# Second batch of the first layer: the transposed normalised input from VectorE, with moments spread as rows

## The chip, the cores and the metric

The kernel runs on one core of a Trainium2 chip. A core has five engines with queues of their own: TensorE (matrix products; the profile splits it into PE, the products, and PEld, the loading of weights), VectorE (DVE), ScalarE (ACT), GpSimd (POOL) and SyncE (SP), which issues nearly all DMA transfers here. Each engine works through its instructions in a fixed order and waits for semaphores. The metric is the device time of one launch in microseconds (us); lower is better.

## What is computed

Two layers over x of shape 4 x 512 x 256 (four batches, 512 tokens, 256 channels), all in float32. The parts that matter here, from the reference:

```python
xn = _layernorm(x)                          # (x - mean) / sqrt(var + 1e-5), per token
s  = _L0_attn_ref(xn, ...)                  # xn + rmsnorm(xn @ M) * norm_w, M made of W_in, W_out and a gain
g  = silu(_L0_ffn_ref(xn, W1, W2, W3))      # W2 . fwht(silu(W1 xn) * (W3 xn))
x  = x + s * g
xn = _layernorm(x)
s  = _L1_attn_ref(xn, ...)                  # a causal attention with a layernorm of its own
g  = silu(_L1_ffn_ref(xn, ...))             # as in the first layer
x  = x + s * g
```

In the first layer's mixer the recurrence is taken over a single step from a zero state, so it collapses into one 256 x 256 matrix M = W_in^T . diag(g) . W_out^T, with g a sum over B and C. The Walsh-Hadamard transform is folded into W2.

## The kernel before

**Arithmetic.** Products keep float32 accuracy by splitting each operand into a high and a low part (`split`, L59: a copy to the high part on ACT, a subtract to the low part on VectorE) and adding three products (`mm3`, L80). Transposes on TensorE are products with an identity in float32 (`transpose`, L77).

**Order of work.** The kernel is written as generators whose steps are handed to the slots of a feed-forward network (FFN). One FFN per layer and batch is the backbone: `ffn` (L466) in the first layer, 8 chunks of 128 hidden units. For each chunk c TensorE forms the up and gate products (tiles f_0gu, f_1gu and so on, the digit is the batch), ACT takes silu, VectorE multiplies (`gates`, L528), the result is split (L539) and the down products (f_0dn) follow. Behind each chunk come two slots (L548, L552), and `Beside` (L884) spreads the steps of the other work over the 16 slots. The order of instructions on each engine is then made by a planner from the written order, which comes with priorities, and a model of the durations; `after(ins)` (L463) binds the instructions of a block to a place behind `ins` on the same engine, without a wait of its own.

**The first batch** differs: its down products all stand behind the up products (defer = NH, L1042), for the W2 of the first layer is still being transformed (`prep_first`, L965) while the up products run. `prep_first` also loads the second batch's x (L981) and makes M (`prep_m`, L191, with tiles wg, wi, mps and m; the split of W_in into wi is L207). Its chunks 0 to 3 write their hidden into early tiles, and the low halves of these four are made later, two behind chunk 6 and two behind chunk 7 (L540 to L544).

**The work around the change.** In the FFN of the first batch the slots carry, in this order (L1007 to L1019): `prep_first` (12 steps left), `mixer(0)` (L716, 3 steps: two banks of xn @ M, then the RMS norm, which starts at L730, and the addition to xn) and `norm(0, 1)` (L430, 3 steps), the layernorm of the second batch:

- `layernorm` (L266): statistics (L275), aggregation (L277), the addition of eps (L279) on VectorE, the power -1/2 on POOL (L280), then xn of 4 token tiles on VectorE (L282).
- for each half k of the channels: 4 transposes of 128 x 128 on TensorE into a bank of PSUM (`transpose_half`, L288, tiles xt_1tp), then a split into the high and the low part of xT. These feed f_1gu, the up products of the second batch.

`first["xt"]` (L459) is the last of these transposes, and the down products of the first batch's chunks 6 and 7 are bound behind it (L559).

**Moments as rows.** The second layer knows another way already: in `norm` with layer = 1 (L436 to L455) `moments` (L254) gives the mean and the reciprocal deviation of each token as a tile mr of 128 x 8, one transpose on TensorE (mrp) turns it to 8 x 128, ACT copies it out (rows), SP writes it to DRAM (there) and reads it back spread over all 128 partitions (mrb, 128 x 2 x 512). VectorE then uses rows of it as operands on a transposed tile.

**Buffers.** Large tiles come from a ring of 10 buffers (`t4`, L44); x and the scratch of W2's transform share 4 (`x_slot`, L96). PSUM has 3 banks for "ms" (mps, o, w2ps, xt_1tp, mrp), 3 for "gu" and 2 for "dn".

Of the kernel before, what the change touches and what calls it, by code (L numbers as in the profile page):

```python
# [21 lines left out]
P = 128  # L22
# [13 lines left out]
def kernel(ctx: ExitStack, tc: tile.TileContext, a: dict, out: bass.AP):  # L36
# [154 lines left out]
    def prep_m(win, wout):  # L191

        cb = wp.tile([P, 4, 2, DS], F32, name="cb")
        nc.vector.tensor_tensor(cb, bc[:, :, 0:2, :], bc[:, :, 2:4, :], ALU.mult)
        cbd = wp.tile([P, 4, DS], F32, name="cbd")
        nc.vector.tensor_tensor(cbd, cb[:, :, 0, :], cb[:, :, 1, :], ALU.subtract)
        g = wp.tile([P, 4], F32, name="g")
        nc.vector.tensor_reduce(g, cbd, AX.X, ALU.add)
        wg = [t4(f"wg{i}", [P, 4, D], F32R) for i in "hl"]
        wi = [t4(f"wi{i}", [P, 4, D], F32R) for i in "hl"]  # L200
        for c in range(4):
            nc.scalar.mul(wg[0][:, c, :], wout[:, c, :], g[:, c : c + 1])
            nc.vector.scalar_tensor_tensor(
                wg[1][:, c, :], wout[:, c, :], g[:, c : c + 1], wg[0][:, c, :].bitcast(F32),
                ALU.mult, ALU.subtract,
            )
        split(win, *wi)  # L207
        yield
        hi, lo = (wp.tile([P, 2, D], F32R, name=f"m{i}") for i in "hl")
        o = psum("mps", [P, 2, D])  # L210
        for i in range(2):
            mm3(
                o[:, i, :],
                [(tuple(z[:, k, sl(i)] for z in wi), tuple(z[:, k, :] for z in wg)) for k in range(4)],
            )
        split(o, hi, lo)
        first["m"] = hi, lo
        yield
# [160 lines left out]
    def norm_first():  # L379
# [47 lines left out]
        first["norm"] = hi_, lo_  # L427
        yield

    def norm(layer, b):  # L430
        xn = act.tile([P, NT, D], F32, tag="xn", name=f"xn{layer}_{b}", bufs=3)
        xns[layer, b] = xn
        with after(first["gate"] if b > 1 - layer else None):
            first["scaled"] = layernorm(f"ln{layer}_{b}", xs[b], xn)
        yield
        if layer:  # L436


            mr = act.tile([P, 2, NT], F32, tag="mr", name=f"mr{b}", bufs=2)
            moments(f"ln2_{b}", xn, mr)  # L440
            yield
            o = psum(f"mrp{b}", [2 * NT, P], **DN[b == 0])
            transpose(o, mr.rearrange("p a t -> p (a t)"), ident)
            rows = act.tile([2 * NT, P], F32, tag="rows", name=f"rows{b}", bufs=1)
            with after(first["table"] if b else None):
                nc.scalar.copy(rows, o)
            there = dram.tile([2 * NT, P], F32, tag="rows", name=f"there{b}")
            nc.sync.dma_start(there, rows)
            mrb = t4(f"mrb{b}", [P, 2, S])
            nc.sync.dma_start(  # L450
                mrb, there.rearrange("(a t) p -> a (t p)", a=2).unsqueeze(0).to_broadcast([P, 2, S])
            )
            mrs[b] = mrb
            yield
            return  # L455
        hi, lo = xTs[0, b] = xt_pair(f"xt0_{b}")
        for k in range(2):
            o = transpose_half(f"xt0_{b}", xn, k)
            first["xt"] = line["last"]  # L459
            split(o, hi[:, k, :], lo[:, k, :])  # L460
            yield
# [4 lines left out]
    def ffn(name, xT, w13, w2, slot, defer=1, spare=(), parts=1, behind=False, tail=()):  # L466

        w2h, w2l = w2
        dn, outs, firsts = [], [], {}

        def down(c, hh, hl, tiles=range(NT)):
            if not dn:
                dn.extend(psum(f"{name}dn{i}", [P, 2, D], tag="dn", bufs=2) for i in range(2))
                outs.extend(dn[t // 2][:, t % 2, :] for t in range(NT))
            for t in tiles:
                o = outs[t]
                for n, (l, r) in enumerate(((hh, w2h), (hh, w2l), (hl, w2h))):  # L480
                    first = c == 0 and n == 0
                    stop = c == NH - 1 and n == 2

                    def one(start):
                        return matmul(
                            o, l[:, sl(t)], r[:, c, :], start=start, stop=stop, skip_group_check=True
                        )

                    if first and t % 2 == 1:
                        with tc.issue_after(firsts[t // 2].ins):
                            ins = one(False)
                    elif first:
                        ins = firsts[t // 2] = one(True)
                    else:
                        ins = one(False)
            return ins

        queue, gates, late = [], [], []  # L500
        for c in range(NH):
            with after(gates[-2] if behind and c >= 2 else None):
                wh, wl = w13(c // 2)
            gu = []
            for j in range(2):

                o = psum(f"{name}gu{c}_{j}", [P, S], **(DN[0] if behind and c == 1 else GU))
                cols = slice((c % 2) * D + j * P, (c % 2) * D + (j + 1) * P)
                gu.append((o, cols))
            for half in range(parts if c == 0 else 1):  # L510
                n = S // (parts if c == 0 else 1)
                ts_ = slice(half * n, (half + 1) * n)
                if parts == 1 or c:
                    for o, cols in gu:
                        last_up = mm3(o[:, ts_], k_pairs((wh, wl), cols, xT, ts_))
                    continue

                for n, (w, x) in enumerate(((wh, xT[0]), (wl, xT[0]), (wh, xT[1]))):
                    for o, cols in gu:
                        for k in range(2):  # L520
                            last_up = matmul(
                                o[:, ts_], w[:, k, cols], x[:, k, ts_],
                                start=n + k == 0, stop=n + k == 3,
                            )
            gu = [o for o, _ in gu]
            h = hid(f"{name}h{c}")
            first["silu"] = nc.scalar.activation(h, gu[0], AF.Silu)
            gates.append(nc.vector.tensor_tensor(h, h, gu[1], ALU.mult))  # L528
            first["gate"] = gates[-1]
            if c < len(spare):  # L530
                hh, hl = spare[c]
            else:
                hh = hid(f"{name}hh{c}", F32R)
                hl = hid(f"{name}hl{c}", F32R)
            if c < len(spare):
                nc.scalar.copy(hh, h)
                late.append((hl, h, hh))
            else:
                split(h, hh, hl)  # L539
            for _ in range(2 if c >= NH - 2 else 0):  # L540
                if late:
                    lo_, h_, hi_ = late.pop(0)
                    with after(gates[-1]):
                        nc.vector.tensor_tensor(lo_, h_, hi_.bitcast(F32), ALU.subtract)  # L544
            queue.append((c, hh, hl))
            ups = last_up if behind else None
            with after(gates[-1] if behind else None), after(ups):
                slot(2 * c)  # L548
            if len(queue) > defer:
                down(*queue.pop(0))  # L550
            with after(gates[-1] if behind else None), after(ups):
                slot(2 * c + 1)  # L552
        line["fixed"] = bool(tail)
        line["last"] = last_up
        for what in tail:
            what()
        for q in queue:

            with after(first.get("xt") if behind and q[0] >= NH - 2 else None):  # L559
                down(*q)  # L560
        return dn

# [153 lines left out]
    def mixer(b):  # L716
# [5 lines left out]
        for i in range(2):  # L722
# [4 lines left out]
            for t in (2 * i, 2 * i + 1):  # L727
                nc.scalar.activation(junk, osb[:, t, :], AF.Square, accum_out=r[:, t : t + 1])
            yield
        nc.vector.tensor_scalar(r, r, 1.0 / D, RMS_EPS, ALU.mult, ALU.add)  # L730
        nc.gpsimd.tensor_tensor(r, r, mhalf, ALU.pow)
        for t in range(NT):
            nc.vector.scalar_tensor_tensor(
# [182 lines left out]
    def call(f, *args):  # L916
        f(*args)
        yield


    NORM, MIXER, W2P = 3, 3, 12

# [82 lines left out]
    for b in range(B):  # L1005
        tasks = []
        if b == 0:  # L1007
            prep = prep_first()
            next(prep)
            tasks.append((prep, 12))  # L1010
        if b:
            tasks.append((call(gate_all, f"g0_{b - 1}", dn, xns[0, b - 1], xs[b - 1]), 1))
        tasks.append((mixer(b), MIXER))
        if b + 1 < B:
            if b:
                load_x(b + 1)
            if b == 2:
                tasks.append((prep_s(0), 4))
            tasks.append((norm(0, b + 1), NORM))  # L1019
        if b == 0:  # L1020
            early = w2_tile("early0"), w2_tile("early1")
            spare = [
# [175 lines left out]
```

## Time and profile before

| | us |
|---|---|
| median of 3 runs | 358.62 (358.52 to 358.67) |
| the profiled execution's own time | 358.58 |
| its span, first to last instruction | 356.8 |
| TensorE busy in it | 351.1 |
| VectorE busy | 287.1 |
| ScalarE busy | 197.8 |
| GpSimd busy | 20.8 |
| mean granted TensorE clock | 0.998 of full speed |

The span is what the trace covers; 1.78 us of the execution's own time lie around it. A busy share is an average over stages. The end of a matmul is modelled, since matmuls overlap in the array: how far apart two of them start says more than how long each is shown. In the tables of instructions in order of time the columns are the start in us, the length in us, the engine, the line, the operation, the written tile <- the read tiles, the shape (for TensorE contraction x output rows, then the moved operand), the count of merged instructions and, in brackets, idle time of the engine before it with what ended it. L70 is the helper through which all products go, so they are told apart by their tiles.

### The profile page before, as it was taken

The numbers are of one execution on the slowest core, as the hardware profiler recorded it, in microseconds if no ns is written. First come the engines' busy times: TensorE is split into PE (matmuls) and PEld (weight loads), VectorE is DVE, ScalarE is ACT, GpSimd is POOL, SyncE is SP. The second block draws the span as 40 slices with busy tenths as digits, with TensorE's granted clock in tenths as the row PEclk, the third lists the DMA queues.
The fourth block names the chain that finished last, engine by engine and source line by source line (L and its number), as shares of the span: only waits on it lengthen the run. The fifth ranks groups of instructions, "written<-read, shape, count | busy, mean of one in ns | idle before, by whom it ended". The sixth has DMA issues, their size and how long they took to land.

```text
span 356.8 us, 6274 instructions
## 1 busy us (share of the span) xinstructions
PE 351.1 (98%) x2477; PEld 327.5 (92%) x2477; DVE 287.1 (80%) x597; ACT 197.8 (55%) x373; POOL 20.8 (6%) x22
## 2 busy tenths in 40 slices
PE   8999999999999999999999999999999999999995
PEld 6878998888988898888999999999999999999994
DVE  6899659998579938998887957989679897577646
ACT  3666166265463425674467655586555676556443
POOL 2000110300020210100110001100011000000000
PEclk9999999999999999999999999999999999999999
DMA  7935000301044316656257145562554745445501
GB/s 232 349 96 201 2 1 2 116 2 61 0 162 168 145 38 229 251 180 195 114 208 263 36 174 208 216 224 93 206 202 150 227 163 206 141 157 184 198 2 59
DMA packets 16284, 52.25 MB, mean 146 GB/s; under 512 B 1632, under 2 KB 7936, under 8 KB 16256
## 3 DMA queue, kind: packets, MB, share of 16 engines
q1 hardware_dynamic: 15968, 51.60, 41.0%
q8 instruction: 19, 0.31, 0.4%
q10 hardware_dynamic: 288, 0.26, 0.2%
q14 instruction: 9, 0.07, 0.1%
HBM read 42.40 MB, written 9.45 MB: 145 GB/s over the span
## 4 chain that ended last, share of the span: by engine, by line
PE 98%; DVE 1%; ACT 0%; issue 0%
PE f_0dn L70 6%; PE f_1dn L70 6%; PE f_2dn L70 6%; PE f_0gu L70 6%; PE f_1gu L70 6%; PE f_2gu L70 6%; PE f_3gu L70 6%; PE f_3dn L70 6%; PE sc L70 4%; PE pv L70 4%; PE o L70 3%; PE v L70 3%; PE tq L70 3%; PE warm L70 2%; PE w2ps L70 1%; PE pt L70 1%
## 5 line engine op out<-in xcount | busy, mean ns | idle before, releaser
L70 PE MATMUL f_3gu<-xt,w 128*128 128x512 f32 x96 | 25.0, 396 | 0.0
L70 PE MATMUL f_2gu<-xt,w 128*128 128x512 f32 x96 | 24.8, 395 | 0.0
L70 PE MATMUL f_1gu<-xt,w 128*128 128x512 f32 x96 | 24.8, 395 | 0.0
L70 PE MATMUL f_0gu<-xt,w 128*128 128x512 f32 (+1 forms) x108 | 24.3, 378 | 0.0
L70 PEld LDWEIGHTS f_0gu<-xt,w 128*128 128x128 f32 x108 | 18.4, 188 | 4.4 <-issue 1.0
L70 PEld LDWEIGHTS f_1gu<-xt,w 128*128 128x128 f32 x96 | 17.0, 188 | 3.1
L70 PEld LDWEIGHTS f_2gu<-xt,w 128*128 128x128 f32 x96 | 17.0, 188 | 3.0
L70 PEld LDWEIGHTS f_3gu<-xt,w 128*128 128x128 f32 x96 | 17.0, 188 | 2.9
L61 ACT CAST f_2hh<-f_2h 128x512 fp32r<-128x512 f32 x16 | 10.0, 622 | 15.4 <-DVE f_2h L528 12.2
L70 PE MATMUL f_3dn<-w2l,f_3hh 128*128 128x256 f32 x64 | 17.7, 281 | 0.0
L70 PE MATMUL f_3dn<-w2h,f_3hh 128*128 128x256 f32 x64 | 17.7, 281 | 0.0
L70 PE MATMUL f_1dn<-w2l,f_1hh 128*128 128x256 f32 x64 | 17.7, 281 | 0.0
L70 PE MATMUL f_2dn<-w2h,f_2hh 128*128 128x256 f32 x64 | 17.7, 282 | 0.0
L70 PE MATMUL f_1dn<-w2h,f_1hh 128*128 128x256 f32 x64 | 17.6, 280 | 0.0
L70 PE MATMUL f_2dn<-w2l,f_2hh 128*128 128x256 f32 x64 | 17.6, 280 | 0.0
L70 PE MATMUL f_3dn<-w2h,f_3hl 128*128 128x256 f32 x64 | 17.0, 281 | 0.0
L70 PE MATMUL f_1dn<-w2h,f_1hl 128*128 128x256 f32 x64 | 17.0, 281 | 0.0
L70 PE MATMUL f_2dn<-w2h,f_2hl 128*128 128x256 f32 x64 | 16.7, 281 | 0.0
L61 ACT CAST f_3hh<-f_3h 128x512 fp32r<-128x512 f32 (+1 forms) x17 | 10.0, 594 | 10.1 <-DVE f_3h L528 5.9
L61 ACT CAST f_1hh<-f_1h 128x512 fp32r<-128x512 f32 x16 | 9.9, 622 | 9.7 <-DVE f_1h L528 6.6
L62 DVE TENSOR_TENSOR f_2hl<-f_2h,f_2hh 128x512 fp32r<-128x512 f32 x16 | 10.9, 684 | 4.5 <-ACT f_2hh L61 4.5
L62 DVE TENSOR_TENSOR f_3hl<-f_3h,f_3hh 128x512 fp32r<-128x512 f32 (+1 forms) x17 | 11.0, 654 | 3.7 <-ACT f_3hh L61 3.6
(487 smaller groups left out, 1147.3 us busy)
## 6 DMA issues: line engine op xcount, KB each, us to landing
sw<-s SPq DMA_DIRECT2D x32, 896.0 KB, 5.7
s<-sp SPq DMA_DIRECT2D x8, 512.0 KB, 4.1
s<-sp SPq DMA_DIRECT2D x8, 384.0 KB, 2.8
w2raw<-in_w SPq DMA_DIRECT2D x4, 512.0 KB, 5.3
sraw<-in_w SPq DMA_DIRECT2D x4, 512.0 KB, 3.2
mrb<-there SPq DMA_DIRECT2D x4, 512.0 KB, 3.6
w13raw<-in_w SPq DMA_DIRECT2D x3, 512.0 KB, 6.8
x<-in_x SPq DMA_DIRECT2D x3, 512.0 KB, 3.5
```

The costliest lines, as they stand in the source:

```text
L61: h = nc.scalar.copy(hi, src)
L62: return h, engine.tensor_tensor(lo, src, hi.bitcast(F32), ALU.subtract)
L70: ins = call(*args, **kwargs)
```

## The change

In the first layer's second batch, xT is no longer made by transposing xn on TensorE. The host hands over a transposed copy of that batch's x (`xT`, 2 x 128 channels on the partitions, 512 tokens). `norm_second` loads it (raw), computes the moments with `moments`, spreads them through `spread`, which is the second layer's code taken out of `norm`, and makes xT on VectorE by one subtract and one multiply over 128 x 1024, then one split. xn itself, which the mixer and the gate read, is still made from x, now behind the split.

The order moves with it: the moments are bound behind the low half of wi (`first["wi"]`), `prep_first`'s last two steps come behind them, and the steps of the mixer and of `norm_second` alternate. `first["xt"]` is now the transpose of the moments, and the down products of chunks 2 to 7 are bound behind it. The last two late low halves are bound behind the moments, the mixer's RMS behind the split (`first["second"]`).

```diff
-        split(win, *wi)
+        first["wi"] = split(win, *wi)[1]
...
+    def spread(name, o):
+
+        rows = act.tile([2 * NT, P], F32, tag="rows", name=f"rows{name}", bufs=1)
+        nc.scalar.copy(rows, o)
+        there = dram.tile([2 * NT, P], F32, tag="rows", name=f"there{name}")
+        nc.sync.dma_start(there, rows)
+        mrb = t4(f"mrb{name}", [P, 2, S])
+        nc.sync.dma_start(
+            mrb, there.rearrange("(a t) p -> a (t p)", a=2).unsqueeze(0).to_broadcast([P, 2, S])
+        )
+        return mrb
+
+    def norm_second():
+
+        x, xn = xs[1], act.tile([P, NT, D], F32, tag="xn", name="xn0_1", bufs=3)
+        xns[0, 1] = xn
+        raw = t4("xTraw", [P, 2, S])
+        nc.sync.dma_start(raw, a["xT"])
+        mr = act.tile([P, 2, NT], F32, tag="mr", name="mr0_1", bufs=2)
+        with after(first["wi"]):
+            moments("ln0_1", x, mr)
+        yield
+        o = psum("mrp0_1", [2 * NT, P])
+        with after(line["last"]):
+            transpose(o, mr.rearrange("p a t -> p (a t)"), ident)
+        first["xt"] = line["last"]
+        mrb = spread("0_1", o)
+        yield
+        hi, lo = xTs[0, 1] = xt_pair("xt0_1")
+        for i, op in enumerate((ALU.subtract, ALU.mult)):
+            row = mrb[:, i, :].unsqueeze(1).to_broadcast([P, 2, S])
+            nc.vector.tensor_tensor(raw, raw, row, op)
+        ins = first["second"] = split(raw, hi, lo)[1]
+
+        for t in range(NT):
+            with after(ins):
+                nc.vector.tensor_scalar(
+                    xn[:, t, :], x[:, t, :], mr[:, 0, t : t + 1], mr[:, 1, t : t + 1],
+                    ALU.subtract, ALU.mult,
+                )
+        yield
...
-                    with after(gates[-1]):
+                    with after(gates[-1]), after(first.get("moments") if c == NH - 1 else None):
                         nc.vector.tensor_tensor(lo_, h_, hi_.bitcast(F32), ALU.subtract)
...
-            with after(first.get("xt") if behind and q[0] >= NH - 2 else None):
+            with after(first.get("xt") if behind and q[0] >= 2 else None):
                 down(*q)
...
-        nc.vector.tensor_scalar(r, r, 1.0 / D, RMS_EPS, ALU.mult, ALU.add)
+        with after(first["second"] if b == 0 else None):
+            nc.vector.tensor_scalar(r, r, 1.0 / D, RMS_EPS, ALU.mult, ALU.add)
...
+    def steps_of(gen, n):
+        for _ in range(n):
+            next(gen)
+            yield
...
-            tasks.append((prep, 12))
+
+            n = norm_second()
+            m = mixer(0)
+            tasks += [(steps_of(prep, 10), 10), (steps_of(n, 1), 1), (prep, 2)]
+            tasks += [(steps_of(g, 1), 1) for g in (m, n, m, n, m)]
         if b:
             tasks.append((call(gate_all, f"g0_{b - 1}", dn, xns[0, b - 1], xs[b - 1]), 1))
-        tasks.append((mixer(b), MIXER))
+            tasks.append((mixer(b), MIXER))
...
-            tasks.append((norm(0, b + 1), NORM))
+            if b:
+                tasks.append((norm(0, b + 1), NORM))
...
+        "xT": v["L0_attn_x"][1].T.reshape(2, P, S).transpose(1, 0, 2),
```

More of the change, by code (lines that the diff above doesn't have):

```diff
@@ L443, in norm @@
             transpose(o, mr.rearrange("p a t -> p (a t)"), ident)
-            rows = act.tile([2 * NT, P], F32, tag="rows", name=f"rows{b}", bufs=1)
             with after(first["table"] if b else None):
[L446 to L453, printed above, removed]
+                mrs[b] = spread(b, o)
             yield
```

## The prediction

> **What bounds the kernel now.** I read the share of each engine first, then the chain of waits, then TensorE, VectorE and the DMA issues in order of time round the change (20 to 60 us).
>
> ```profile
> PE   8999999999999999999999999999999999999995
> DVE  6899659998579938998887957989679897577646
> PE 98%; DVE 1%; ACT 0%; issue 0%
> ```
>
> The first two lines give tenths busy in 40 slices of 8.9 us, the third is the chain that ended last. TensorE works in every slice between its first instruction at 1.45 us and its last at 352.25 us, and the table by stretches (8 to 36.3, 36.3 to 51.1, and on to 352.6 us) has it busy 344.53 of 344.60 us. So the time is TensorE's queue, pitch after pitch: what leaves that queue is gained, and any wait that enters it is lost. No other engine's busy time counts while TensorE still finds ready work.
>
> **Removed: eight transposes of xn on TensorE.** In order of time (start, length, engine):
>
> ```profile
> 47.19 0.28 PE L70 MATMUL f_0dn<-w2h,f_0hl 128*128 128x256 f32 x1
> 47.31 1.04 PE L70 MATMUL xt_1tp<-ident,xn 128*128 128x128 f32 x8
> 48.10 0.37 PE L70 MATMUL f_0dn<-w2h,f_0hh 128*128 128x256 f32 x1
> 48.30 0.28 PE L70 MATMUL f_0dn<-w2l,f_0hh 128*128 128x256 f32 x1
> ```
>
> Matmuls overlap, so starts are compared. Products 128x256 start every 0.12 us; without the transposes the product at 48.30 would have started at 47.43. The eight cost 0.87 us, as the chain also has it (0.87 for x8).
>
> **Added on TensorE: one transpose of the moments,** 128x8 weights against the identity. The second layer has the same instruction:
>
> ```profile
> 129.56 0.27 PE L70 MATMUL mrp<-ident,mr 128*8 128x128 f32 x1
> 129.58 0.48 PE L70 MATMUL o<-mh,xt 128*128 128x256 f32 x2
> 129.90 0.28 PE L70 MATMUL o<-ml,xt 128*128 128x256 f32 x1
> ```
>
> Without it the third product would start at 129.56 + 2 x 0.12 = 129.80; it starts at 129.90, so 0.10. At 229.30 us five products behind it end 0.12 later than five without it. I take 0.11. TensorE's balance is -0.87 + 0.11 = -0.76 us. All other products are the same in number and shape.
>
> The Trainium skill, "VectorE: DVE Perf Modes", section "Rules for kernel authors", speaks against the change: a 128x128 transpose belongs on TensorE when PSUM will do as its target. The section "The three transpose paths" there gives 390 ns for one in bf16; by that figure the balance would be -8 x 0.39 + 0.39 = -2.7 us, an estimate. The row shows 0.109 us each in a full queue, and that decides.
>
> **Moved: the moments.** Mean and variance of the second batch go from behind VectorE's queue of the up products to directly behind wil, the low half of W_in:
>
> ```profile
> 30.32 1.21 DVE L62 TENSOR_TENSOR wil<-win,wih 128x1024 fp32r<-128x1024 f32 x1
> 34.46 1.39 DVE L275 BATCH_NORM_STATS2 ln_1st<-x 128x6 f32<-128x256 f32 x4
> 40.23 0.16 DVE L279 TENSOR_SCALAR ln_1r<-ln_1mv 128x4 f32<-128x4 f32 x1
> 41.51 1.38 DVE L282 TENSOR_SCALAR xn<-x,ln_1mv,ln_1r 128x256 f32<-128x256 f32 x4 [1.12 <-POOL ln_1r L280]
> 48.08 0.17 DVE L730 TENSOR_SCALAR ssr<-ssr 128x4 f32<-128x4 f32 x1 [5.18 <-ACT junk L728]
> ```
>
> x1 is issued at 21.32 and a load like it lands within 4.5 us, so it is there by 26 us, before wil ends at 31.53. The moments cost 1.39 (statistics) + 0.5 (four aggregations of 0.158, overlapped) + 0.25 (copy 0.16 and add 0.16, overlapped) = 2.1 us and would end near 33.6; the power on POOL (1.01) near 34.7. The 1.39 were already in front of the last w2l and the last gate; what is new in front of the gates is about 0.7 us, and 2.1 us in front of the sixth gate and the first two late low halves. What waits for these: the third products (hl) of the down matmuls for chunks 0 to 3. Cover: the first and second products of chunks 0 to 3, 4 x 8 x 0.118 = 3.8 us, need no low half of the hidden. So I price the delay at 0; without that cover it is 2.1.
>
> **Added: the way round through memory.** The rows are copied (0.26 on ACT), written to DRAM and read back, spread over 128 partitions, both on SP. Issues in the second layer:
>
> ```profile
> 130.15 0.34 SPq L448 DMA_DIRECT2D there<-rows  x1
> 131.38 0.35 SPq L450 DMA_DIRECT2D mrb<-there  x1
> 183.67 0.28 SPq L448 DMA_DIRECT2D there<-rows  x1
> 186.78 0.33 SPq L450 DMA_DIRECT2D mrb<-there  x1
> DMA to landing us min/median/max: 3.3/3.6/3.8
> ```
>
> The read waits for the write: 1.23 us here, 3.11 there (3.05 and 3.02 in the other two). The last line, of mrb, is issue to landing. So 4.5 to 6.9 us from the write's issue to mrb in SBUF. "DMA: Bandwidth & Descriptors", section on latency and the DMA's two cost components, puts some 2.0 us of fixed cost on every transfer plus bytes by 436 GB/s, hence 2.0 + 3.2 = 5.2 us for the two as an estimate; the rows reach further and are used.
>
> On SP nothing but the loads for later batches stands around it: x2, x3 and two w2raw are issued from 24.52 to 30.43 us, and then nothing before 65.90. The new load of the transposed x (512 KB) goes in the same stretch, beside x1; the DMA engines move 2 GB/s from 36 to 51 us, so the spread travels alone. Of the ten t4 buffers, raw and mrb take two more; the four of wg and wi come free when the last mps product ends at 36.1, before mrb needs one. A w2raw that comes later for it is not read before 56.89. Price 0; if such a load stood in front of mrb, one landing of w2raw, at most 6.4 us (its own row), would be added to mrb.
>
> **Added on VectorE:** subtract and multiply over 128x1024. Nearest rows: tensor with tensor on 128x1024, 1.21 to 1.22 us, so 2.4 with the second overlapped; a spread row read with a zero step is shown at 128x512 (0.68 to 0.69 with mrb) and costs no more than a plain one. The split becomes one copy on ACT (wih, 1.03) and one subtract (1.22) instead of two of 0.59 and two of 0.69 with PSUM sources: nothing saved, nothing lost. They fall in the hole between 42.89 and 48.08, where VectorE waits 5.18 us for the mixer's squares. The four xn instructions (1.38) move behind them, and the mixer's ssr (48.08) behind that low half; the mixer's tail is read by the gates at 53.0 us, so it has some us to spare. Price 0.
>
> **When it arrives.** With mrp at 34.8 us: rows out at 35.4, mrb at 40.0 to 42.5, difference and product to 44.9, the high half near 46.1, the low half near 47.4. TensorE wants them when the last down product is through: 51.02 - 0.76 = 50.3. From mrp to the high half the chain is 0.6 + 4.5 to 6.9 + 2.4 + 1.1 + some 0.2 of handing over = 8.8 to 11.2 us, so mrp must start by 39 us (slow memory) or 41.5 (fast). I expect 34.8 to 38, and so no wait.
>
> **Sum.** Against the profiled execution, 358.58 (span 356.8 and 1.78 around it): 358.58 - 0.87 + 0.11 = 357.82; the median of the runs is 0.04 higher, which gives **357.86 us**, 0.21% less.
>
> **Rivals.** (a) *The spread comes late,* the slower side. If the moments stay where they ended before (power done at 41.48), mrp starts at 41.6; until then the rule that chunks 2 and up wait behind mrp leaves TensorE only chunks 0 and 1 (done at 39.0) and the mixer's first bank (1.4 us), a wait of 1.2. Then the high half is ready at 52.8 at worst, while 6 x 1.42 us of down products and 1.4 of the mixer run to 51.5: 1.3 more. 357.86 + 2.5 = 360.4. It decides from mrp later than 39. For it: VectorE stands at 9 in both slices before 36 us. Against: the order behind wil is fixed in the code. Chance 0.16. (b) *The gates starve TensorE* at 36 us: moments ahead of low halves, 2.1 us with the 3.8 of cover gone: 359.96. Against it: the high products are many. Chance 0.05. (c) *The gain is handed back:* TensorE arrives 0.76 us earlier at a later stage where VectorE (9 tenths in the 7th to 9th and the 13th and 14th slice) or a load sets the pace, or waits some tenths for the low half: 358.1 to 358.6. Against it: 0.07 us idle in 344.6 shows stages with work in hand. Chance 0.12. (d) *The transposes remain in effect,* that is mrp plus its wait cost as much as the eight: 358.6, contained in (c).
>
> **How the numbers follow.** The forecast has 0.67. The predicted time is its time. Its own spread is 357.7 to 358.1: mrp 0.10 to 0.12, and an occasional tenth of waiting. A change of 0.2% (0.72 us, so 357.90) is about what can be told from none here, and the forecast lies just beyond it: 0.53 of its 0.67 falls under 357.90, 0.14 above. From (c) all 0.12 is "same"; of (a) and (b) 0.03 ends within the bound and 0.18 beyond it. Faster 0.53, same 0.29, slower 0.18. The range goes down to 357.6 (transposes out, mrp free, and a tenth or two of spread) and up to 359.2, half way into (a).
>
> **What would show it.** xt_1tp gone from the second batch's rows in the first layer and mrp once more, with TensorE still without idle time between 31 and 52 us. mrp before 38 us; mrb landing before 43; the low half before 49. A wait of TensorE in front of mrp, of the second chunk's down products or of the first f_1gu is (a); one near 36 us in front of a product with a low half is (b). Were TensorE's first f_1gu 0.76 us earlier and the end not, it is (c). The prediction is wrong if the spread's DMAs take over 9 us, or if the moments do not follow wil.

## The result, and the profile after

The changed kernel takes **361.50 us** (median of 6 runs, 361.21 to 362.15) against 358.58 before (6 runs, 358.35 to 358.67): a ratio of 1.0083, 95% interval 1.0073 to 1.0094. The prediction said 357.86 with a range up to 359.2; the change costs 2.9 us where it should have gained 0.7. The profiled execution has a span of 359.9 us (356.8 before). All profiled executions here and below had the full granted TensorE clock from 8 us to the last product, except that of e4_no_hop (363.30 us, 0.50 from 43.0 to 46.3 us), so its later rows are not compared in time.

The page first: busy tenths of TensorE and VectorE in 40 slices of 9.0 us, and the chain that ended last.

```profile
PE   7999899999999999999999999999999999999995
DVE  6899448999579956898897967989769897568645
PE 79%; DVE 14%; DMA 3%; issue 1%; POOL 1%; ACT 1%; SPq 0%; POOLq 0%
```

TensorE alone made up 98% of the chain before; now VectorE, a DMA and GpSimd are on it. In the fifth slice (36 to 45 us) TensorE falls to 8, and VectorE stands at 4 in the fifth and sixth, where its hole has grown. The places are found in TensorE's rows in order of time (start, length, and in brackets the idle time before and who ended it):

```profile
40.08 0.28 PE L70 MATMUL o<-mh,xt 128*128 128x256 f32 x1
41.39 0.27 PE L70 MATMUL mrp<-ident,mr 128*8 128x128 f32 x1 [1.03 <-POOL mr L264]
...
51.34 0.27 PE L70 MATMUL f_0dn<-w2h,f_0hl 128*128 128x256 f32 x1
52.37 1.20 PE L70 MATMUL f_1gu<-xt,w 128*128 128x512 f32 x4 [0.75 <-ACT xt L61]
...
68.93 0.38 PE L70 MATMUL f_1dn<-w2h,f_1hl 128*128 128x256 f32 x1 [0.36 <-DVE f_1hl L62]
74.25 0.38 PE L70 MATMUL f_1dn<-w2h,f_1hl 128*128 128x256 f32 x1 [0.85 <-DVE f_1hl L62]
```

Four waits, where before there was none after 1.45 us. (The page lists a fifth idle time, 0.74 in front of xt_0tp at 6.30, behind warm-up products. It costs nothing: before, that transpose came at 6.31.) What each costs is read from starts, since products are 0.28 long but start every 0.12: mrp should have come at 40.20 and came at 41.39 (1.19 lost), the first f_1gu at 51.46 and came at 52.37 (0.91), the two f_1dn lose 0.52 and 1.00. Each loses 0.16 more than the idle time in brackets, which is the overlap of two products. With the balance of the transposes: -0.76 + 1.19 + 0.91 + 1.52 = +2.86 us; the medians differ by 2.92. Up to the first f_1gu the sum holds to 0.01: it comes 1.35 later than before.

That the sum also fits at the end is partly luck, for it leaves out three things. Behind three of the waits the next product comes 0.10 late as well. The last 1471 products, the same in the same order, take 181.50 us before (170.75 to 352.25) and 181.19 in the changed kernel (173.98 to 355.17), 0.31 less, and much the same in every kernel below (181.12 to 181.22); why is open. And from the start of the last product to the end of the span it is 4.77 in place of 4.54. So the loss is these four waits; what the sum leaves out is 0.2 to 0.3 each time, and not all of one sign.

Then the rows that feed mrp, VectorE's, GpSimd's, SyncE's and ScalarE's:

```profile
30.34 1.22 DVE L62 TENSOR_TENSOR wil<-win,wih 128x1024 fp32r<-128x1024 f32 x1
31.47 1.40 DVE L259 BATCH_NORM_STATS2 ln_1st<-x 128x6 f32<-128x256 f32 x4
...
36.45 0.30 DVE L261 BATCH_NORM_AGGREGATE ln_1mv<-ln_1st 128x2 f32<-128x6 f32 x3
36.67 0.66 DVE L62 TENSOR_TENSOR f_0hl<-f_0h,f_0hh 128x512 fp32r<-128x512 f32 x1
37.24 0.68 DVE L62 TENSOR_TENSOR ml<-mps,mh 128x512 fp32r<-128x512 f32 x1
37.84 0.68 DVE L562 TENSOR_TENSOR f_0h<-f_0h,f_0gu 128x512 f32<-128x512 f32 x1
38.44 0.16 DVE L262 COPY mr<-ln_1mv 128x4 f32<-128x4 f32 x1
38.51 0.16 DVE L263 TENSOR_SCALAR mr<-ln_1mv 128x4 f32<-128x4 f32 x1
38.58 1.29 DVE L578 TENSOR_TENSOR early<-f_0h,early 128x512 fp32r<-128x512 f32 x2
39.78 0.68 DVE L62 TENSOR_TENSOR f_0hl<-f_0h,f_0hh 128x512 fp32r<-128x512 f32 x1
...
38.75 2.58 POOL L264 TENSOR_TENSOR mr<-mr,mhalf 128x4 f32<-128x4 f32 x1 [31.96 <-DVE mr L263]
...
41.98 0.36 SPq L435 DMA_DIRECT2D there<-rows  x1
44.47 0.35 SPq L437 DMA_DIRECT2D mrb<-there  x1
...
48.75 2.48 DVE L461 TENSOR_TENSOR xTraw<-xTraw,mrb 128x1024 f32<-128x1024 f32 x2 [8.28 <-DMA mrb<-there]
51.27 1.05 ACT L61 CAST xt<-xTraw 128x1024 fp32r<-128x1024 f32 x1 [6.47 <-DVE xTraw L461]
```

Only the statistics stand directly behind wil. Between them and the add at 38.51 are two weight splits, low halves, gates and ml, so the moments end at 38.67, 5.1 us later than the 33.6 of the prediction. The power, 1.01 us in the kernel before, where VectorE stood idle beside it, then takes 2.58 beside the late low halves. mr is there at 41.33, mrp starts, mrb lands near 48.7, the high half is out at 52.32.

### The profile page after: what moved, and what is told of

It reads as the page before. It is cut to its first block, busy times and chain, and to the rows that moved or that the text cites. A ratio compares the mean times of both kernels' runs of the same rounds, so it can differ in the third digit from the quotient of the medians.

```text
span 359.9 us, 6264 instructions
## 1 busy us (share of the span) xinstructions
PE 350.3 (97%) x2470; PEld 325.4 (90%) x2470; DVE 288.7 (80%) x599; ACT 197.6 (55%) x373; POOL 25.9 (7%) x22
## 4 chain that ended last, share of the span: by engine, by line
PE 79%; DVE 14%; DMA 3%; issue 1%; POOL 1%; ACT 1%; SPq 0%; POOLq 0%
PE f_2dn L70 6%; PE f_2gu L70 6%; PE f_3gu L70 6%; PE f_3dn L70 6%; PE f_1dn L70 5%; PE sc L70 4%; PE pv L70 4%; PE v L70 3%; PE f_0dn L70 3%; PE tq L70 3%; PE f_1gu L70 2%; PE o L70 2%; DVE w2b L155 1%; DVE w2b L156 1%; DVE f_0h L562 1%; PE pt L70 1%
## 5 line engine op out<-in xcount | busy, mean ns | idle before, releaser
L62 DVE TENSOR_TENSOR f_2hl<-f_2h,f_2hh 128x512 fp32r<-128x512 f32 x16 | 10.9, 684 | 3.9 <-ACT f_2hh L61 3.8
```

The lines of the kernel that those rows point to most:

```text
L62: return h, engine.tensor_tensor(lo, src, hi.bitcast(F32), ALU.subtract)
```

## The experiments

Every kernel below is the changed kernel with the edit shown, timed against the kernel before on the same chip. The expectations name theories by letters. A: the moments come late from VectorE's queue. B: work of VectorE that piles up behind 52 us makes the f_1dn waits. D: the power is slow because of what VectorE runs beside it. Idle time in front of xt_0tp, which costs nothing, is left out of the last column (0.74 in the changed kernel, 0.26 in e5, 0.56 in e10).

| run | median us | ratio to before (95%) | power us | TensorE's waits (idle us) |
|---|---|---|---|---|
| changed kernel | 361.50 | 1.0083 (1.0073 to 1.0094) | 2.58 | mrp 1.03, f_1gu 0.75, f_1dn 0.36 + 0.85 |
| e1_tight | 360.34 | 1.0046 (1.0029 to 1.0063) | 1.38 | o 0.44, f_2dn 0.49, f_3dn 0.34 |
| e2_tail | 362.71 | 1.0120 (1.0105 to 1.0135) | 2.58 | mrp 1.04, f_1gu 1.62, f_2dn 0.20, f_3dn 0.73 |
| e3_quiet | 360.69 | 1.0072 (1.0044 to 1.0100) | 1.01 | f_1gu 0.99, f_1dn 0.86 |
| e4_no_hop | 361.74 | 1.0098 (1.0077 to 1.0119) | 3.72 | mrp 2.62, f_2dn 0.48, f_3dn 0.36 |
| e5_lows | 358.47 | 1.0000 (0.9990 to 1.0009) | 1.98 | o 0.44 |
| e6_tight_n2 | 360.48 | 1.0051 (1.0034 to 1.0068) | 1.38 | f_0gu 0.94, f_2dn 0.48, f_3dn 0.48 |
| e7_lows_n2 | 360.64 | 1.0058 (1.0043 to 1.0073) | 1.01 | f_0gu 0.94, f_2dn 0.48, f_3dn 0.48 |
| e8_tight_tail | 360.37 | 1.0054 (1.0039 to 1.0069) | 1.38 | o 0.44, f_2dn 0.21, f_3dn 0.72 |
| e9_three | 360.08 | 1.0045 (1.0032 to 1.0057) | 1.01 | o 0.34, f_2dn 0.49, f_3dn 0.52 |
| e10_three_b | 358.58 | 0.9999 (0.9990 to 1.0008) | 1.01 | f_1dn 0.63 |
| e11_three_b_xn | **357.77** | **0.9975 (0.9964 to 0.9985)** | 1.01 | none |
| e12_lows_xn | 358.42 | 0.9995 (0.9986 to 1.0004) | 1.98 | o 0.44 |

**e1_tight: the moments directly behind wil.** Late hidden low halves, late gates and the second weight split of half 1 are bound behind the moments.

```diff
-                split(o, w2h[:, qs, ds_], w2l[:, qs, ds_])
+                with after(first.get("moments") if layer == 0 and half else None):
+                    split(o, w2h[:, qs, ds_], w2l[:, qs, ds_])
...
+            with after(first.get("moments") if behind and c >= 6 else None):
                 gates.append(nc.vector.tensor_tensor(h, h, gu[1], ALU.mult))
...
+                with after(first.get("moments") if behind and c >= 5 else None):
                     split(h, hh, hl)
```

> On VectorE the low half of W2 and of chunk 5 and the gates from chunk 6 on are bound behind the moments, so these are done soon after wil. Theory A (the loss comes from the moments being finished late, at 41.3 us, and everything behind them late): the power ends by 37, the moments' transpose starts by 37.5 without a wait of TensorE of its own, the spread rows land by 45, the first up product of the second batch has no wait, and the backlog of VectorE behind it is gone too: 357.8 to 358.2 us. Rival B (the way through DRAM is too long wherever it starts): the first up product still waits, 360 or more. Rival C (VectorE's extra work starves TensorE at the down products of the first batch once the gates stand behind the moments): new waits for low halves near 36 to 40 us, 359 to 361.

Measured 360.34. The add ends at 34.24, the power at 35.71, mrp (37.81) and the first f_1gu wait for nothing, and the f_1dn waits are gone: late moments are what made the waits before mrp and f_1gu. The time is missed by 2, because the plan put other work in other places; it lies in the range of rival C, but the waits are not the ones that C named. TensorE's rows that now wait:

```profile
35.82 0.50 PE L70 MATMUL o<-mh,xt 128*128 128x256 f32 x2 [0.44 <-ACT mh L61]
...
114.33 0.39 PE L70 MATMUL f_2dn<-w2h,f_2hl 128*128 128x256 f32 x1 [0.49 <-DVE f_2hl L62]
...
171.27 0.39 PE L70 MATMUL f_3dn<-w2h,f_3hl 128*128 128x256 f32 x1 [0.34 <-DVE f_3hl L62]
```

**e2_tail: the mixer's tail and xn freed.** xn is made right behind the spread's issue, and the mixer's RMS no longer waits for the split.

```diff
         mrb = spread("0_1", o)
+        for t in range(NT):
+            nc.vector.tensor_scalar(
+                xn[:, t, :], x[:, t, :], mr[:, 0, t : t + 1], mr[:, 1, t : t + 1],
+                ALU.subtract, ALU.mult,
+            )
...
-        with after(first["second"] if b == 0 else None):
-            nc.vector.tensor_scalar(r, r, 1.0 / D, RMS_EPS, ALU.mult, ALU.add)
+        nc.vector.tensor_scalar(r, r, 1.0 / D, RMS_EPS, ALU.mult, ALU.add)
```

> xn of the second batch is made as soon as its moments are there, and the mixer's RMS is no longer bound behind the split, so the mixer's tail can use VectorE's idle stretch of 8.3 us before the rows land. Theory A': the two waits of the second batch's down products for low halves (1.5 us from start to start) come from this tail being pushed behind 52 us: they vanish, while the wait for the moments (1.2) stays and that of the first up product (0.9) stays or grows by up to 1: 360.0 to 361. Rival: these two waits come from something else (the later load of the next layer's W2, the long powers on GpSimd): they stay, 361.5 or more.

Measured 362.71: slower, not faster. Both f_1dn waits go, as B has it, but the wait before f_1gu doubles (1.62). VectorE's rows show why: of the tail, osb (46.13) was done before mrb landed, but the addition to xn (49.56) went between subtract (48.42) and multiply (50.70), and on ScalarE the gates' silu (50.97) went in front of the high half (52.16). The order that the change fixed here, split first and tail behind it, kept that wait shorter (0.75).

**e3_quiet: VectorE stands still during the power.** One xn tile, which reads the power's result, is put right behind the moments, and the last two late low halves and that of chunk 7 behind it.

```diff
             moments("ln0_1", x, mr)
+        with after(first["moments"]):
+            first["quiet"] = nc.vector.tensor_scalar(
+                xn[:, 0, :], x[:, 0, :], mr[:, 0, 0:1], mr[:, 1, 0:1], ALU.subtract, ALU.mult
+            )
...
-                    with after(gates[-1]), after(first.get("moments") if c == NH - 1 else None):
+                    with after(gates[-1]), after(first.get("quiet") if c == NH - 1 else None):
```

> VectorE makes one tile of xn directly behind the moments, so that it stands still until GpSimd has made the power; the last two late low halves and that of chunk 7 come behind. Theory D (GpSimd's power takes 2.58 us instead of 1.01 because VectorE runs instructions with two SBUF inputs meanwhile): the power takes 1.0 to 1.1, ends near 39.8, TensorE's wait for it vanishes (-1.2) and that of the first up product shrinks to about 0.5: 359.7 to 360.3. Rival (the power is slow by its form or by being the first in a long time): it takes 2.5 again, and as VectorE stands still meanwhile the time is 361.5 or more.

Measured 360.69. VectorE and GpSimd:

```profile
38.63 0.16 DVE L263 TENSOR_SCALAR mr<-ln_1mv 128x4 f32<-128x4 f32 x1
39.92 0.42 DVE L452 TENSOR_SCALAR xn<-x,mr 128x256 f32<-128x256 f32 x1 [1.12 <-POOL mr L264]
...
38.88 1.01 POOL L264 TENSOR_TENSOR mr<-mr,mhalf 128x4 f32<-128x4 f32 x1 [32.27 <-DVE mr L263]
```

The add ends where it did in the changed kernel, the power is back at 1.01, and the wait before mrp is gone: D is shown, and with it that 1.57 of the lateness came from the power. The wait before f_1gu stays (0.99): the copy of the rows stood behind the mixer's squares on ScalarE (41.55), so the write left at 41.82, 0.16 earlier only.

**e4_no_hop: no way round through memory.** mrb is loaded early from x. This kernel leaves out that xT depends on the moments, so it computes something else.

```diff
-        mrb = spread("0_1", o)
+        nc.scalar.copy(act.tile([2 * NT, P], F32, tag="rows", name="rows0_1", bufs=1), o)
+        mrb = t4("mrb0_1", [P, 2, S])
+        nc.sync.dma_start(
+            mrb, a["x"][0, 0:4, :].rearrange("(a t) p -> a (t p)", a=2).unsqueeze(0).to_broadcast([P, 2, S])
+        )
```

> The spread rows are loaded early from x itself instead of from the moments (a part of the computation is replaced, so the result is another): no way through DRAM, the rest as in the changed kernel. Theory A: the wait for the moments' transpose (1.2 us) stays, since the down products are still bound behind it; the wait of the first up product (0.9) vanishes, and with VectorE's work no longer late most of the later 1.5: 359.0 to 359.5. If the way through DRAM has no part in the loss: 361.3 or more.

Measured 361.74. There is no wait before f_1gu (the high half is out at 48.42, the first f_1gu comes at 54.44), so the memory's way was that wait's last link. But subtract and multiply, now free to go, ran right behind the late low halves, and the power got slower still. VectorE, GpSimd, TensorE:

```profile
38.89 1.29 DVE L582 TENSOR_TENSOR early<-f_0h,early 128x512 fp32r<-128x512 f32 x2
40.10 0.68 DVE L62 TENSOR_TENSOR f_0hl<-f_0h,f_0hh 128x512 fp32r<-128x512 f32 x1
40.70 1.22 DVE L465 TENSOR_TENSOR xTraw<-xTraw,mrb 128x1024 f32<-128x1024 f32 x1
...
39.06 3.72 POOL L264 TENSOR_TENSOR mr<-mr,mhalf 128x4 f32<-128x4 f32 x1 [32.42 <-DVE mr L263]
...
42.84 0.37 PE L70 MATMUL mrp<-ident,mr 128*8 128x128 f32 x1 [2.62 <-POOL mr L264]
```

The power waits until the subtract ends (41.92) and is done 0.86 later; the multiply, which needs the subtract's result, follows at 41.95 and does not hold it. Taking one cost away made another larger, so this run does not give the price of the way through memory.

**e5_lows: one part alone.** All four late low halves behind the moments, not the last two.

```diff
-                    with after(gates[-1]), after(first.get("moments") if c == NH - 1 else None):
+                    with after(gates[-1]), after(first.get("moments")):
```

> One part alone: all four late low halves of batch 0's gated outputs wait behind the moments (before, the last one only), everything else as in the changed kernel. Theory A (the queue in front of the add makes the moments late, the power beside VectorE's two-input work makes them later): the add moves from 38.51 to about 37.0, the power runs beside the four low halves and takes 2.5 to 3.2, ends near 39.9, mrp waits 0 to 0.3 in place of 1.03, and the first f_1gu comes 0.9 to 1.3 earlier than in the changed kernel, with no wait or a short one in front of it. The two f_1dn waits (1.21 in all) stay, since VectorE's backlog behind 52 us is the same: 359.9 to 360.6. Rival (the wait in front of the first f_1gu is set by the rows' way through memory and by VectorE's two passes, not by when the moments end): the wait in front of f_1gu stays at 0.75 and the time stays at 361 or above.

Measured **358.47**, the kernel before. The add moves from 38.51 to 36.12, mrp from 41.39 to 38.60, and the f_1gu wait is gone as A says; that the f_1dn waits go with it was not expected: with mrb at 44.84 in place of 48.75, VectorE is through with split, xn and tail 4 us earlier. So B is not a second cause here, but the late moments once more. What is left is one wait of TensorE that costs time:

```profile
36.19 1.28 DVE L578 TENSOR_TENSOR early<-f_0h,early 128x512 fp32r<-128x512 f32 x2
37.39 0.68 DVE L62 TENSOR_TENSOR ml<-mps,mh 128x512 fp32r<-128x512 f32 x1
...
36.35 1.98 POOL L264 TENSOR_TENSOR mr<-mr,mhalf 128x4 f32<-128x4 f32 x1 [29.79 <-DVE mr L263]
...
36.84 0.51 PE L70 MATMUL o<-mh,xt 128*128 128x256 f32 x2 [0.44 <-ACT mh L61]
```

Two down products only stand between the last mps product and o, where mh needs its copy (36.20 to 36.78) first. That costs 0.61 before o and 0.11 behind it: just what the transposes had gained.

**e6_tight_n2 and e7_lows_n2: mrp ahead of the mixer.** e6 is e1_tight, e7 is e5_lows with the gated low halves bound from the sixth chunk on, both with

```diff
-            tasks += [(steps_of(g, 1), 1) for g in (m, n, m, n, m)]
+            tasks += [(steps_of(g, 1), 1) for g in (n, m, m, n, m)]
```

> The tight queue of e1_tight, and the normalisation steps of batch 0's neighbour taken one place earlier in the order of tasks (n, m, m, n, m in place of m, n, m, n, m), so that mrp stands right behind the mps products and ahead of the down products o. Theory A: the wait of 0.44 in front of o<-mh at 35.82 goes, mrp waits at most 0.3 on the power (which ended at 35.71 in e1_tight), the first f_1gu comes without a wait near 51.0. If the waits of e1_tight in batches 2 and 3 (0.49 and 0.34) belong to VectorE's total load they stay: 359.5 to 360.0. If they belong to that plan's order alone they go: 358.6 to 359.1. Rival (the change can't win because VectorE's added 5 us come back as waits somewhere, whatever the order): 360.0 or above, with waits on f_hl of 1.2 or more in all.

> As e6_tight_n2, but the bounds are on the low halves (gated outputs' from the sixth chunk on, and all four late ones) in place of on the gates and the second layer's weights; the last weight split of half 1 stays between the statistics and the aggregations. Theory A: add near 34.5 to 35.0, the power beside ml and hl near 1.5 to 2.0, so mrp, which stands right behind the mps products, waits 0.3 to 1.2; the first f_1gu comes without a wait (the way through memory has room). 359.3 to 360.3, and the waits on f_hl tell, against e6_tight_n2, whether they follow the order or the load.

Measured 360.48 and 360.64: e6 in the range of its rival (360.0 or above), e7 above its range. No wait at mrp, o or f_1gu in either; but the plan now puts the last chunk's up products right behind mps, where they wait 0.94 for ScalarE's silu to free their bank, and the two waits on f_2hl and f_3hl stay. That they stay in both settles little between load and order. e5 above and e10 to e12 below do, with the same load on VectorE and neither wait.

**e8_tight_tail: e1 and e2 together.**

```diff
+                with after(first.get("moments") if behind and c >= 5 else None):
                     split(h, hh, hl)
...
-        with after(first["second"] if b == 0 else None):
-            nc.vector.tensor_scalar(r, r, 1.0 / D, RMS_EPS, ALU.mult, ALU.add)
+        nc.vector.tensor_scalar(r, r, 1.0 / D, RMS_EPS, ALU.mult, ALU.add)
```

> e1_tight and e2_tail together: moments directly behind wil, and batch 0's mixer tail and xn freed of the split so that VectorE can do them in its hole from 40 to 44 us. Theory A and B (late moments; backlog behind 52 us): no wait in front of mrp, no f_1dn waits, and since the tail now has VectorE's hole before mrb lands, no wait of more than 0.5 in front of the first f_1gu; what VectorE takes off the time behind 52 us (about 3 us of xn and tail) also takes away the waits at 114 and 171 of e1_tight: 358.2 to 359.3. Rival (the waits at 114 and 171 have nothing to do with the backlog at 52): they stay at 0.3 to 0.7 each and the time is 359.5 to 360.4. Rival 2 (the plan again puts the tail between subtract and multiply, as in e2_tail): a wait of over 1 in front of f_1gu, 360.5 or above.

Measured 360.37, its first rival: with the tail done 3.4 us earlier than in e1 (51.1 in place of 54.5), the waits at 114 and 171 us are still there (0.21 and 0.72). So the backlog at 52 us is not what makes them. In e1_tight's rows VectorE takes an attention sum's split (sp, 0.93 at 112.62) in front of the low half that TensorE waits for; in e5_lows the low half of that stretch (111.40) goes ahead of sp (113.54). That it is this order that decides is read from the rows and was not tried by itself.

**e9_three and e10_three_b: three of the four low halves.** Binding the last three of the four puts 14 down products in front of o<-mh. Both have this; e9 has the bound on low halves from the seventh chunk too.

```diff
-                    with after(gates[-1]), after(first.get("moments") if c == NH - 1 else None):
+                    with after(gates[-1]), after(first.get("moments") if len(late) < 3 else None):
...
-                split(o, w2h[:, qs, ds_], w2l[:, qs, ds_])
+                with after(first.get("moments") if layer == 0 and half else None):
+                    split(o, w2h[:, qs, ds_], w2l[:, qs, ds_])
```

> Built on e5_lows: three of batch 0's four late low halves wait behind the moments (the first goes ahead of them), and so do the second weight split of half 1 and the gated outputs' low halves from the seventh chunk on. By the plan 14 down products now stand between the mps products and o<-mh, so that mh has 1.7 where it needs 0.6. Theory A: the wait of 0.44 that e5_lows still had in front of o<-mh at 36.84 (0.6 to 0.7 with the restart) goes; the add ends near 35.7, the power takes 1.4 to 2.0 and ends at or before mrp's place near 37.9; the first f_1gu comes 0.6 to 0.75 earlier than in e5_lows with no wait; the time is 357.6 to 358.0, that is 0.5 to 1.0 below the kernel before: what the eight transposes are worth. Rival (the waits on low halves at f_1dn, f_2dn or f_3dn come and go with each plan, since VectorE has no room left from 55 to 120 us): one or two of 0.3 to 0.8 appear, and the time is 358.2 to 359.0.

> As e9_three without the bound on the gated outputs' low halves: one more of them stands in front of the add, which ends near 36.3; the power ends near 37.9 to 38.2, about where mrp stands. Theory A: a wait of 0 to 0.3 in front of mrp, no wait in front of o<-mh and f_1gu: 357.6 to 358.3. Rival as in e9_three: 358.2 to 359.0, with waits on low halves at f_1dn, f_2dn or f_3dn.

e9 misses both its ranges at 360.08: mrp has no wait, but o's second bank waits 0.34 for the copy of the rows, and the plan is one of those with waits at 114 and 171 us. e10 gives 358.58, its rival's time. Its first f_1gu comes at 50.31, 0.71 before the 51.02 of the kernel before, and one wait takes it back. The kernel before, then e10:

```profile
51.02 0.63 PE L70 MATMUL f_1gu<-xt,w 128*128 128x512 f32 x2
...
50.31 1.09 PE L70 MATMUL f_1gu<-xt,w 128*128 128x512 f32 x4
...
71.20 0.39 PE L70 MATMUL f_1dn<-w2h,f_1hl 128*128 128x256 f32 x1 [0.63 <-DVE f_1hl L62]
```

VectorE made that low half at 70.45, and was busy without a gap from 60 to 80 us (10.00 of 10 us in each half). It was so in e5 too, which has no such wait; what counts is how much stands in front of the low half.

**e11_three_b_xn and e12_lows_xn: VectorE's hole used.** e10_three_b and e5_lows, with xn freed as in e2_tail, but the mixer's tail left behind the split.

```diff
         mrb = spread("0_1", o)
+        for t in range(NT):
+            nc.vector.tensor_scalar(
+                xn[:, t, :], x[:, t, :], mr[:, 0, t : t + 1], mr[:, 1, t : t + 1],
+                ALU.subtract, ALU.mult,
+            )
...
-        for t in range(NT):
-            with after(ins):
-                nc.vector.tensor_scalar(
...
```

> e10_three_b, with batch 1's four xn tiles freed of the split, so that VectorE makes them in its hole from 40 to 45.5 us (1.38 of work) and not behind it at 50.3; the mixer's tail stays where it is. In e10_three_b the first f_1gu came at 50.31 (0.71 before the one of the kernel before), and all of that was lost again in one wait of 0.63 on f_1hl in front of f_1dn at 71.2. Theory B (that wait is VectorE's backlog behind 52 us): the low half it waits for comes 1.3 earlier, the wait goes and none takes its place: 357.7 to 358.0, 0.6 to 0.9 below the kernel before. Rival (the backlog is filled by whatever is next in the plan, and the low half stays where it is): the wait stays at 0.4 or more and the time at 358.3 to 358.7.

> e5_lows, with batch 1's four xn tiles freed of the split in the same way. e5_lows had no wait on a low half but one of 0.44 on mh in front of o, which the plan leaves in place here. Theory B: freeing VectorE changes nothing on the path, since no wait on VectorE was left: 358.3 to 358.6, with the same wait of 0.44 at o<-mh and no others. Rival (VectorE's 1.38 us are worth something by themselves): 358.0 or below.

Both came as theory B said. e12, which had no wait on VectorE to lose, stays at 358.42 with its 0.44 before o. e11 has no wait of TensorE left behind 1.45 us and takes **357.77 us, 0.25% less than the kernel before** (ratio 0.9964 to 0.9985). VectorE and TensorE of e11:

```profile
40.14 1.37 DVE L459 TENSOR_SCALAR xn<-x,mr 128x256 f32<-128x256 f32 x4
45.41 2.48 DVE L467 TENSOR_TENSOR xTraw<-xTraw,mrb 128x1024 f32<-128x1024 f32 x2 [3.29 <-DMA mrb<-there]
69.20 0.68 DVE L62 TENSOR_TENSOR f_1hl<-f_1h,f_1hh 128x512 fp32r<-128x512 f32 x1
...
38.00 0.27 PE L70 MATMUL mrp<-ident,mr 128*8 128x128 f32 x1
50.21 1.09 PE L70 MATMUL f_1gu<-xt,w 128*128 128x512 f32 x4
```

xn lies in the hole, the low half comes at 69.20 in place of 70.45, and the wait is gone. It is faster than both kernels of this study.

## Why the prediction was wrong

**Removed and added on TensorE: right.** Net -0.76 was predicted. The first f_1gu comes 0.71 (e10) and 0.81 (e11) earlier than before; e10 started its mps products 0.06 later than the kernel before and e11 0.03 earlier, so both gain 0.77 to 0.78 with the same products in front. e11, in which nothing waits, takes 0.88 less by the medians. The predicted 357.86 is about the time of the change once its order is mended (357.77); that the two lie within 0.1 is partly luck, for the 0.3 that the last 1471 products regain and the 0.23 more at the end of the span were not in the sum and nearly cancel.

**Moved, the moments: the step that failed.** It said they follow wil and end at 33.6, the power at 34.7. They ended at 38.67 and 41.33. Two things were wrong. "The order behind wil is fixed in the code" is true of what the moments wait for, not of what waits for them: only the last two late low halves were bound behind them, and the planner filled the 5.1 us with splits, gates and low halves. And the power was taken at the 1.01 of a row where VectorE stood idle; it took 2.58. e1 takes away nearly all of the first (add done at 34.24), e5 nearly half of it (36.28), e3 all of the second, and in each the wait at mrp goes. The prediction itself had named the case: "if the moments do not follow wil".

**The way round through memory: right.** 41.98 to about 48.7, 6.7 us, within 4.5 to 6.9. Issue to landing of mrb is 4.3 in the changed kernel and 5.5 in e10 and e11, longer than the 3.3 to 3.8 of the second layer. Two loads of w2raw follow it by 0.45 us in all three, so these alone do not explain the 5.5; what does is open. The prediction's estimate of 5.2 for both transfers rests on a fit that the page it names gives for transfers issued from GpSimd, while these are SP's; from the write's issue to the subtract they took 5.6 (e8) to 6.9 (e10).

**When it arrives: right as a threshold.** mrp had to start by 39 us with slow memory; it started at 41.39, and the chain to the high half took 10.9 us (8.8 to 11.2 were given). e10 and e11 with mrp at or near 38 do not wait.

**Rival (a) is what happened,** at 1.19 + 0.91 where 1.2 + 1.3 were worked out. It was given 0.16 because the code's order was taken as an answer to "VectorE stands at 9 in both slices before 36 us"; that line should have weighed more.

**Added on VectorE: priced 0; in the changed kernel 1.52,** by e5 a consequence of the late moments. Nothing was wrong with the durations (2.48, 1.05, 1.23). But "the mixer's tail has some us to spare" named no figure. It ran until 59.5, and VectorE was then full up to 90 us, so what had slipped out of the hole came back as the two f_1dn waits. This is what puts the result above (a)'s 360.4. With the moments in time the slip is smaller: none in e5, 0.63 of idle time in e10, none once xn is in the hole (e11).

**Rivals (b) to (d):** (b) did not occur; (c) is e5 and e10, the gain handed back by one short wait; (d), mrp and its wait costing as much as the eight, was true of the changed kernel (1.19 + 0.1 against 0.87) as a part of (a), and falls with e11.

Open is why some plans (e1, e2, e4, e6 to e9) have waits on f_2hl and f_3hl and others (the changed kernel, e3, e5, e10 to e12) have none; the rows point to where the planner puts the attention sums in front of a low half, and no run moved those alone.

## What to carry to other kernels

A bound that says "this after that" does not say "this next": list what else the planner may put in between on that engine, and bind those behind it if the result is on the path. When TensorE has no slack, a gain of 0.8 us is settled by single waits of half a microsecond, so price the engine that receives the work by what stands behind it for the next 20 us and not by the hole it is meant for. Moving one bound reshuffles the whole plan, so compare the waits of the new trace one by one before a theory is dropped over the total.

## What the runs showed of the hardware

The power on GpSimd over 128x4 takes 1.01 us alone, and up to 3.72 if it starts while VectorE runs an fp32 TENSOR_TENSOR with both inputs in SBUF. It is then held until that instruction ends, and in these rows until the end of an unbroken row of them, and ends 0.86 to 0.88 us behind it:

| run | power starts | last such VectorE instruction ends | power ends |
|---|---|---|---|
| e6_tight_n2 | 34.19 | 34.70 (f_0hl) | 35.57 |
| e5_lows | 36.35 | 37.47 (early) | 38.33 |
| changed kernel | 38.75 | 40.46 (f_0hl) | 41.33 |
| e4_no_hop | 39.06 | 41.92 (subtract) | 42.78 |
| e11, second power at 67 us | 67.02 | 69.88 (f_1hl) | 70.74 |

A row does not always count as one. In the kernel before, the power at 103.60 is done at 105.51, 0.86 behind the first of two such instructions (sp, over at 104.65), though f_2hl follows at 104.56. Of the 28 powers over 128x4 in these 14 traces that met two or more such instructions in a row, 13 were held to the end of the row and 15 by the first alone; what decides is open.

Instructions with one input in PSUM (w2l, ml, the gate) do not hold it: in e10 it ran in 1.01 from 36.42 beside w2l, and the early low half that began at 36.83 took its usual 0.70. The Trainium skill, "SBUF — State Buffer", section "Who interferes with whom", has the rule: a VectorE instruction with two SBUF inputs contends with a GpSimd instruction that reads SBUF, since its second input comes through a read interface that both share. These rows agree, and add that a row of instructions without a gap can count as one. The section calls the shared ports an exclusive lock; in e10's row, with GpSimd first, VectorE was not held. The prediction should have weighed this rule against its 1.01.
